# Expert rows fetched five units ahead into the row table's own tiles, half-block pairs ended one unit sooner, and the expert stage's pools laid out anew

## The chip, the cores and the metric

The kernel runs on one core of a Trainium2 chip. The time is the device time of one execution in microseconds. The kernel before was timed three times: 1548.76, 1552.86 and 1553.0 us, median 1552.86. The profile shown below comes from a further execution of 1552.57 us, with a span of 1550.8 us from its first to its last instruction; the profile's times count from the start of the span. TensorE is called PE, VectorE DVE, ScalarE ACT, GpSimd POOL and SyncE SP; SP issues most of the DMAs.

## The reference

The network has two layers on 2708 nodes with 256 features. Each layer is a graph attention, in layer 0 followed by causal self-attention, and then a mixture of eight experts in which every row goes to the two experts with the highest router probability. The expert part is what the change touches:

```python
h1 = jnp.einsum('nc,ehc->neh', flat, w1)
h3 = jnp.einsum('nc,ehc->neh', flat, w3)
h = jax.nn.silu(h1) * h3                       # hidden size 682
y = jnp.einsum('neh,ech->nec', h, w2)
out = jnp.einsum('ne,nec->nc', gates, y)       # gates: two non-zero per row, they sum to 1
x = x + out
```

Everything is computed in float32. The kernel computes only the two chosen experts of each row.

## The kernel before

**Order of the stages.** `network` calls `first` (graph attention, self-attention and routing of layer 0), `experts_blocks(0)`, `second` (graph attention and routing of layer 1) and `experts_blocks(1)`. In `first` and `second` the order of the instructions on each engine is written out by a planner (the class `Plan`, with lengths and ranks given for each step) and is kept as written. In `experts_blocks` the framework orders them: it goes through the program with estimated durations and, on each engine, takes the first instruction in program order whose needs it thinks are met. An engine, or a DMA queue, then works strictly in that order, and the order can differ from the program's by a whole expert.

**The table of rows.** `XR` holds 22 tiles of 128 rows. A row has 268 numbers: 256 features (`XB` is a view of these), the row's token number, eight gates and padding. While a layer is routed, each tile of `XR` is scattered to a table `xs` in DRAM (line 1808, by POOL, twice, once for each chosen expert). There every expert has its own region, with its rows packed in blocks of 128. When the last tile is scattered, `XR` has no more use until the next layer's routing, apart from the first few tiles: some blocks are worked on inside `first` and `second` while the routing still runs (`EARLY`: three blocks in layer 0, four in layer 1; `LATE`: two blocks of layer 0's last expert, worked on at the start of `second`). These early and late blocks are fetched into `XR[:, 0]` and the tiles after it, and run in `some_blocks` (lines 531 to 614).

**Units of an expert stage.** Each expert has five blocks (`NB`), which are worked on in units: a pair, a pair and a single block. Rows beyond five blocks are rare; they are cut in half blocks of 64 rows (`HALF_B`), and ten such half blocks of any experts (`MORE`) run as five half-block pairs, each one unit ahead of the pairs of experts 2 to 6. Which expert a half block belongs to is known only at run time: `table()` computes it on DVE, and SP reads it into registers for the fetch of its rows (line 2023) and for the load of its weights. In units, an expert in the middle of the stage is: half-block pair, pair, pair, single. Layer 0 has 14 pairs and 7 single blocks left for its stage, layer 1 has 15 and 6; the half-block pairs are 5 each.

**A unit, step by step.**

- `fetch` (lines 2023 and 2027): SP brings the unit's rows from `xs` to tiles `xt`, of which there are nine.
- `front` (lines 2041 to 2046): PE transposes the rows to PSUM, ACT copies them to `xTs`.
- `up` (lines 2061 to 2071): for six chunks of the hidden size, PE multiplies the transposed rows by w1 and w3 into a PSUM tile `pup` (five banks), ACT takes the silu of one half (`sl`), DVE multiplies it by the other into `hT`. Five chunks are 128 wide, the last has only 42 columns of each weight. There are three `hT` tiles.
- `down` (lines 2080 to 2086), one unit later: PE multiplies `hT` by w2 into a bank `y` (there are two), DVE multiplies by the gate into `ys`, and POOL adds the rows to the result in DRAM by an indirect accumulating DMA (`add_rows`, line 614). An add waits for the one before it.
- In a pair, the last chunks of the two blocks lie at partitions 0 to 63 and 64 to 127 of `hT`, and the last rows of w2 are loaded twice, so that the two last products each take 64 rows of PE (line 2083).
- A half-block pair does the same in `up_halves` (line 2099; rows 0 to 63 with one room's weights, 64 to 127 with another's), where a gate `gk` is computed with the product `gj` (line 2111) from the rows `xt` alone. Its hidden values come out untransposed (`hid`); `turn_halves` transposes them (line 2121) at the end of the next unit, and `down_halves` (line 2133) runs a unit after that and ends with two adds of 64 rows.

**Weights.** An expert's weights fill a room of 17 KB per partition. Three rooms rotate among the eight experts (two in `arena`, one called `room`), and two more (`more`) take the weights of a half-block pair. `load_expert` (lines 1983 to 1990) issues seven DMAs, three of 640 KB and four of 42 KB; the first use of a room also clears its padding on POOL (1975, 1976).

**Order of the work in the stage's loop.** For unit k the program emits: the load of an expert's room, the load of the two extra rooms (three units after a half-block pair began), the fetch of unit k + 2, the unit's own `up` or `up_halves`, the turn of an earlier half-block pair, the front of unit k + 2 and the down of unit k - 1.

**Where the tiles lie.** Pools of tiles stack in SBUF. After `arena` comes a place which the stages use in turn. In bytes per partition from there: in `first`, `X0` to 22.5 KB, the attention's pool to 78 KB, then a pool with the early blocks' `xTs` and `ys` to 95 KB; in `second`, `X1` to 22.5 KB, a pool `skeep` to 56 KB, and a pool `swork` with the blocks' `xTs`, `chunks` and `ys` to 95 KB. In `experts_blocks` the pool with `hT`, the three rooms and the small table tiles comes first, to 71.5 KB, and the pool with `xt`, `xTs`, `sl`, `ys` and `hid` follows to 101 KB. A tile may be written only when what lay in its place is no longer in use.

The two lines that say which rows a fetch takes and where it puts them are

```python
xt = sp.tile([P, ROW], F32, tag="xt", name="xt", bufs=9)
after_all(nc.sync.dma_start(out=xt, in_=xs[row:row + P, :]), xs)
```

where `after_all` makes the fetch wait for all scatters of the layer.

Of the kernel before, what the change touches and what calls it, by code (L numbers as in the profile page):

```python
# [24 lines left out]
NT = (N + P - 1) // P  # L25
# [5 lines left out]
NE = 8  # L31
HID = 682
NHC = (HID + P - 1) // P
HH = HID // 2
NF = HID // P
# [4 lines left out]
HALF_B = 64  # L40
MORE = 10
# [107 lines left out]
def adj_ffn_kernel(ctx, tc, x, adj, vecs, bias_rows, tab, w_gnn0, w_gnn1, wqkv, wo,  # L149
# [43 lines left out]
    make_identity(nc, ident)  # L193
    offdiag = const.tile([P, P], F32, name="offdiag")
# [1218 lines left out]
    def second(X, XB, xs0, x1, x2, sd, mb, xs, arena, load_weights):  # L1413
# [9 lines left out]
        with ExitStack() as s:  # L1423
# [8 lines left out]
            identb = keep.tile([P, P], BF16, name="identb")  # L1432
            nc.vector.tensor_copy(identb, ident)
# [537 lines left out]
    def load_expert(room, w1, w3, w2, e, used=False):  # L1971
        cut = NF * P
        a, b, c, d = weights_at(room)
        if not used:
            nc.gpsimd.memset(c, 0.0)
            nc.gpsimd.memset(d[:, NF, :], 0.0)
        if isinstance(e, int):
            w1v, w3v = (w[:, e, :].rearrange("(k p) h -> p k h", p=P) for w in (w1, w3))
            w2v = w2[e]
        else:  # L1980
            w1v, w3v = (w[:, bass.ds(e, 1), :].rearrange("(k p) o h -> p k (o h)", p=P) for w in (w1, w3))
            w2v = w2[bass.ds(e, 1)].rearrange("o h c -> (o h) c")
        nc.sync.dma_start(out=a, in_=w1v[:, :, :cut])
        nc.sync.dma_start(out=b, in_=w3v[:, :, :cut])
        nc.sync.dma_start(out=c[:, :, :REST], in_=w3v[:, :, cut:])
        nc.sync.dma_start(out=c[:, :, HIGH:], in_=w1v[:, :, cut:])
        nc.sync.dma_start(out=d[:, :NF, :], in_=w2v[:cut, :].rearrange("(k p) c -> p k c", p=P))

        for q in (0, HIGH):
            nc.sync.dma_start(out=d[q:q + REST, NF, :], in_=w2v[cut:, :])  # L1990

    def experts_blocks(layer, w1, w3, w2, xs, acc, arena):
# [8 lines left out]
        with ExitStack() as s:  # L2001
            keep = s.enter_context(tc.tile_pool(name=f"bkeep{layer}", bufs=1))
            hTs = [keep.tile([P, NHC, 2, P], F32, name=f"hT{i}") for i in range(3)]
            for hT in hTs:
                nc.gpsimd.memset(hT[:, NF, :, :], 0.0)
# [3 lines left out]
            with tc.tile_pool(name=f"slot{layer}", bufs=2) as sp, \  # L2009
                    tc.tile_pool(name=f"bpu{layer}", bufs=5, space=PSUM) as pu, \  # L2010
# [5 lines left out]
                def fetch(unit):  # L2016
                    xts = []
                    for e, j in unit:
                        xt = sp.tile([P, ROW], F32, tag="xt", name="xt", bufs=9)
# [30 lines left out]
                def up(k, w, xT, B):  # L2050

                    hT = hTs[k % len(hTs)]
                    for n in range(NHC):
                        pp = pu.tile([P, 2, 2, P], F32, tag="pp", name="pup")
# [12 lines left out]
                        else:  # L2067
                            nc.scalar.activation(sl[:REST, :B, :], pp[HIGH:HIGH + REST, 0, :B, :], AF.Silu)
                            for b in range(B):
                                q = HIGH * b  # L2070
                                nc.vector.tensor_tensor(hT[q:q + REST, n, b, :], sl[:REST, b, :],
                                                        pp[:REST, 0, b, :], ALU.mult)
                    return hT

                def down(e, w, hT, xts):

                    ys = [bank() for _ in xts]
                    for b, y in enumerate(ys):
                        for n in range(NF):
                            nc.tensor.matmul(y, hT[:, n, b, :], w[3][:, n, :], start=(n == 0), stop=False)  # L2080
                    for b, y in enumerate(ys):
                        part_ = slice(HIGH * b, HIGH * (b + 1)) if len(ys) > 1 else slice(0, P)
                        nc.tensor.matmul(y, hT[part_, NF, b, :], w[3][part_, NF, :], start=False, stop=True)  # L2083
# [106 lines left out]
                xt = [fetch(u) for u in units[:2]]  # L2190
                nxt = [front(x) for x in xt[:2]]
                asked, more_asked = 1, 0
                turns, downs = {}, {}
                for k, unit in enumerate(units):
                    e = unit[0][0]

                    if k == 0 or e is not None and e + 2 < NE and asked < e + 2 and units[k - 1][0][0] == e:
                        asked += 1
                        load_expert(rooms[asked % 3], w1, w3, w2, asked, asked > 2)
                    if k == 1:  # L2200
                        table()
                    if k == 2 or k > 2 and units[k - 3][0][0] is None and more_asked < MORE:
                        for room in more_rooms:
                            load_expert(room, w1, w3, w2, register(tab[0:1, 0, more_asked:more_asked + 1], NE - 1), more_asked > 1)
                            more_asked += 1
                    if k + 2 < len(units):
                        xt.append(fetch(units[k + 2]))
# [184 lines left out]
```

## Time and profile before

| What | Value |
|---|---|
| Time, median of three runs | 1552.86 us (1548.76 to 1553.0) |
| Time of the profiled execution | 1552.57 us |
| Its span, mean granted PE clock | 1550.8 us, 0.97 |
| Busy in the span: PE, DVE, ACT, POOL | 92%, 49%, 37%, 34% |
| First and last up product of layer 0's expert stage | 513.68 and 830.1 us |
| First and last up product of layer 1's expert stage | 1198.96 and 1522.7 us |
| DMA, mean over the span | 131 GB/s |

A page of the profile gives busy times and shares, the span in 40 slices of equal length (each digit is the busy share of a slice in tenths), the chain of work that ended last and the costliest groups of instructions. A line of the timeline has the start, the duration, the engine, the line of the kernel, the operation and the tiles written and read, and in brackets the time for which the engine had been idle and what ended it. A line of the waits has the instruction that waited, what it waited for, the total, the number of times and the longest. Where an instruction needed several things, the wait is put down to the one that came last.

### The profile page before, as it was taken

What the parts mean: (1) busy time and instruction counts of PE and PEld (TensorE: products, weight loads), DVE (VectorE), ACT (ScalarE), POOL (GpSimd) and SP (SyncE); (2) the same over time, 40 slices, a digit from 0 to 9 for tenths busy, and PEclk for the clock granted to TensorE, in tenths of its full rate; (3) what the DMA queues carried; (4) which work ended last, traced back from release to release, by engine and by line L of the source; (5) the groups of instructions that cost most, each with busy time, mean ns of one, the idle gap of its engine ahead of it and who ended that gap; (6) DMA issues with size and microseconds to landing.
All of it is one profiled execution on the core that took longest, in us unless ns stands there. A gap on an engine that the chain in (4) does not pass through costs nothing. (4 is left out here: it accounts for less than half of the span.)

```text
span 1550.8 us, 21255 instructions
## 1 busy us (share of the span) xinstructions
PE 1430.0 (92%) x7488; PEld 1025.5 (66%) x7488; DVE 760.8 (49%) x1670; ACT 566.8 (37%) x1134; POOL 530.9 (34%) x687
## 2 busy tenths in 40 slices
PE   6788898999999899989997899999997999999994
PEld 5533433433437687877786778888767877777883
DVE  5778999956684222221221564767654222122221
ACT  3577776764543122221221453443431212121210
POOL 5677679681063021212122210030444012211221
PEclk9999999999999899999999999999998999999998
DMA  7589667410013653565522751451413737454411
GB/s 262 191 280 303 224 222 230 163 60 8 7 58 92 191 149 104 143 179 168 135 30 43 170 113 34 99 125 48 151 58 99 227 98 205 138 161 121 111 25 19
DMA packets 200537, 203.40 MB, mean 131 GB/s; under 512 B 93752, under 2 KB 170536, under 8 KB 197712
## 3 DMA queue, kind: packets, MB, share of 16 engines
q1 hardware_dynamic: 175798, 172.51, 36.0%
q0 software_dynamic: 20352, 25.85, 9.4%
q10 hardware_dynamic: 4270, 3.58, 0.7%
q8 instruction: 61, 1.00, 0.3%
q14 instruction: 56, 0.46, 0.1%
HBM read 130.01 MB, written 56.37 MB: 120 GB/s over the span
## 5 line engine op out<-in xcount | busy, mean ns | idle before, releaser
L2061 PE MATMUL pup<-xTs,arena 128*128 128x256 f32 (+2 forms) x1320 | 257.9, 354 | 10.3 <-DVE hT L2066 9.6
L2061 PEld LDWEIGHTS pup<-xTs,arena 128*128 128x128 f32 (+1 forms) x1320 | 220.8, 191 | 43.5 <-DVE hT L2066 11.2
L1581 PE MATMUL po<-hb,PT 128*128 128x257 f32 (+2 forms) x968 | 226.0, 387 | 3.2 <-DVE PT L1574 3.2
L2065 ACT ACTIVATE sl<-pup 128x256 f32<-128x256 f32 (+1 forms) x210 | 73.2, 350 | 393.5 <-PE pup L2061 359.9
L1581 PEld LDWEIGHTS po<-hb,PT 128*128 128x128 f32 (+2 forms) x968 | 176.0, 188 | 42.1 <-issue 12.7
L2066 DVE TENSOR_TENSOR hT<-sl,pup 128x256 f32<-128x256 f32 (+1 forms) x210 | 77.6, 379 | 203.5 <-ACT sl L2065 197.3
L1103 ACT ACTIVATE e<-stt 128x1024 f32<-128x1024 f32 (+1 forms) x132 | 125.6, 986 | 94.8 <-PE stt L1097 65.6
L1142 DVE TENSOR_TENSOR es<-es,e 128x1024 f32<-128x1024 f32 x104 | 136.5, 1312 | 29.4 <-ACT e L1103 21.9
L614 POOL DMA_INDIRECT out<-ys,xt x41 | 63.0, 1536 | 252.1 <-DVE ys L2086 146.3
L614 POOL DMA_INDIRECT acc<-ys,xt x40 | 61.7, 1543 | 248.7 <-DVE ys L2086 149.3
L1097 PE MATMUL stt<-qT,kT 64*128 64x512 f32 (+1 forms) x528 | 132.8, 612 | 5.2 <-ACT e L1103 4.6
L1808 POOL DMA_INDIRECT xs<-XR,place x88 | 93.1, 1058 | 91.5 <-DVE mk L1568 39.2
L1123 PE MATMUL o<-e,V 128*64 128x512 f32 (+1 forms) x528 | 123.0, 589 | 0.0
L2080 PE MATMUL y<-arena,hT 128*128 128x256 f32 x510 | 115.2, 380 | 1.1 <-DVE ys L2086 1.1
L1559 ACT ACTIVATE E<-sb,dcol 128x768 f32<-128x768 f32 (+1 forms) x88 | 75.3, 860 | 110.9 <-DVE PT L1574 109.1
L2061 PE MATMUL pup<-xTs,room 128*128 128x256 f32 (+3 forms) x528 | 104.3, 354 | 5.5 <-DVE hT L2066 5.5
L2086 DVE TENSOR_SCALAR ys<-y,xt 128x256 f32<-128x256 f32 x71 | 31.7, 480 | 152.6 <-PE y L2083 152.5
L2080 PEld LDWEIGHTS y<-arena,hT 128*128 128x128 f32 x510 | 94.7, 190 | 13.7 <-DVE ys L2086 1.9
L2061 PEld LDWEIGHTS pup<-xTs,room 128*128 128x128 f32 (+1 forms) x528 | 87.3, 193 | 19.0 <-DVE hT L2066 6.3
L1097 PEld LDWEIGHTS stt<-qT,kT 64*128 64x128 f32 x528 | 44.5, 187 | 78.0 <-issue 63.4
L1123 PEld LDWEIGHTS o<-e,V 128*64 128x64 f32 x528 | 32.9, 137 | 70.1 <-issue 53.7
L971 DVE MAX8 tops<-arena 128x8 f32<-128x2708 f32 (+1 forms) x22 | 65.3, 2969 | 1.2 <-DMA arena<-in_adj 1.2
(322 smaller groups left out, 2088.7 us busy)
## 6 DMA issues: line engine op xcount, KB each, us to landing
more<-in_w SPq DMA_DIRECT2D x60, 640.0 KB
arena<-in_adj SPq DMA_DIRECT2D x21, 1354.0 KB
arena<-in_w SPq DMA_DIRECT2D x36, 640.0 KB
mb<-mb SPq DMA_DIRECT2D x44, 352.0 KB
xt<-xs SPq DMA_DIRECT2D x71, 134.0 KB
xs<-none SPq DMA_DIRECT2D x16, 536.0 KB
room<-in_w SPq DMA_DIRECT2D x12, 640.0 KB
more<-in_w SPq DMA_DIRECT2D x80, 42.0 KB
```

Source lines behind the costliest of these rows:

```text
L614: nc.gpsimd.indirect_dma_start(out=acc[:, :], out_offset=bass.IndirectOffsetOnAxis(ap=tokens.bitcast(I32), axis=0), in_=ys, in_offset=None ...
L1097: nc.tensor.matmul(st[:r, g, c0(sb):], kT[a:b, sb * P:sb * P + r], qT[a:b, t0 + (sb == t0 + 1):t0 + 2, :, :], start=True, stop=True)
L1103: nc.scalar.activation(e[:r, :, c0(sb):], v[sb, "st"][:r, :, c0(sb):], AF.Exp, scale=1.0 / HD ** 0.5)
L1123: nc.tensor.matmul(v["o"][g * HD:(g + 1) * HD, c:], V[:r, sb, g * HD:(g + 1) * HD], v[sb][:r, g, c:], start=(n + i == 0), stop=(n + i == t ...
L1142: nc.vector.tensor_tensor(es, es, v[sb][:r, :, c:], ALU.add)
L1559: nc.scalar.activation(e[:q, :n], sb[:q, i0:i1], AF.Exp, bias=dcol[:q, j:j + 1], scale=SLOPE - 1.0)
L1581: nc.tensor.matmul(v["po", i][:r, :F], v["PT", j][:q, a:a + r], hb[:q, j, :], start=(j == 0), stop=(j == NT - 1))
L1808: i = nc.gpsimd.indirect_dma_start(out=xs[:, :], out_offset=bass.IndirectOffsetOnAxis(ap=at, axis=0), in_=src, in_offset=None)
L2061: nc.tensor.matmul(pp[:to, i, :B, :], wn[:, c, :], xT[:, c, :B, :], start=(c == 0), stop=(c == KC - 1))
L2065: nc.scalar.activation(sl[:, :B, :], pp[:, 0, :B, :], AF.Silu)
L2066: nc.vector.tensor_tensor(hT[:, n, :B, :], sl[:, :B, :], pp[:, 1, :B, :], ALU.mult)
L2080: nc.tensor.matmul(y, hT[:, n, b, :], w[3][:, n, :], start=(n == 0), stop=False)
```

## The change

- `fetch` has no tiles of its own any more. It puts the rows into `XR[:, 5]` to `XR[:, 21]` in rotation, seventeen tiles.
- At the start three units are fetched, at unit 1 (after `table()`) units 3 to 5, and from then on unit k + 5 at unit k.
- The two extra rooms are loaded from unit 1 on, and again two units after a half-block pair began. These loads stand ahead of an expert's own load.
- A half-block pair is turned inside the next unit, between the third and the fourth chunk of its up products, and its `down_halves` runs at the end of that unit.
- In a pair the last chunk is no longer split: both blocks' last chunks lie at partitions 0 to 41, DVE multiplies them in one instruction, and each of the two last down products takes all 128 rows of PE, in a row with the other five. The second copy of w2's last rows is not loaded.
- The pool with `xTs`, `sl`, `ys` and `hid` is opened first and also holds the `hT` tiles; the pool with the rooms and the small tiles follows. The padding of `hT` is cleared on DVE, not on POOL.
- `identb`, used in `second`, is made once at the start and lies with the constants.

```diff
+    identb = const.tile([P, P], BF16, name="identb")
+    nc.vector.tensor_copy(identb, ident)
...
-            identb = keep.tile([P, P], BF16, name="identb")
-            nc.vector.tensor_copy(identb, ident)
...
-        for q in (0, HIGH):
-            nc.sync.dma_start(out=d[q:q + REST, NF, :], in_=w2v[cut:, :])
+        nc.sync.dma_start(out=d[:REST, NF, :], in_=w2v[cut:, :])
...
+            sp = s.enter_context(tc.tile_pool(name=f"slot{layer}", bufs=2))
+            hTs = [sp.tile([P, NHC, 2, P], F32, name=f"hT{i}", bufs=1) for i in range(3)]
+            for hT in hTs:
+                nc.vector.memset(hT[:, NF, :, :], 0.0)
             keep = s.enter_context(tc.tile_pool(name=f"bkeep{layer}", bufs=1))
-            hTs = [keep.tile([P, NHC, 2, P], F32, name=f"hT{i}") for i in range(3)]
-            for hT in hTs:
-                nc.gpsimd.memset(hT[:, NF, :, :], 0.0)
...
+            ring = [XR[:, t, :] for t in range(AHEAD, NT)]
...
-                        xt = sp.tile([P, ROW], F32, tag="xt", name="xt", bufs=9)
+                        xt = ring.pop(0)
+                        ring.append(xt)
...
-                def up(k, w, xT, B):
+                def up(k, w, xT, B, between):
 
                     hT = hTs[k % len(hTs)]
                     for n in range(NHC):
+                        if n == NHC // 2:
+                            between()
...
-                            for b in range(B):
-                                q = HIGH * b
-                                nc.vector.tensor_tensor(hT[q:q + REST, n, b, :], sl[:REST, b, :],
-                                                        pp[:REST, 0, b, :], ALU.mult)
+                            nc.vector.tensor_tensor(hT[:REST, n, :B, :], sl[:REST, :B, :], pp[:REST, 0, :B, :], ALU.mult)
...
                     for b, y in enumerate(ys):
-                        for n in range(NF):
-                            nc.tensor.matmul(y, hT[:, n, b, :], w[3][:, n, :], start=(n == 0), stop=False)
-                    for b, y in enumerate(ys):
-                        part_ = slice(HIGH * b, HIGH * (b + 1)) if len(ys) > 1 else slice(0, P)
-                        nc.tensor.matmul(y, hT[part_, NF, b, :], w[3][part_, NF, :], start=False, stop=True)
+                        for n in range(NHC):
+                            nc.tensor.matmul(y, hT[:, n, b, :], w[3][:, n, :], start=(n == 0), stop=(n == NHC - 1))
...
-                xt = [fetch(u) for u in units[:2]]
+                xt = [fetch(u) for u in units[:3]]
                 nxt = [front(x) for x in xt[:2]]
                 asked, more_asked = 1, 0
-                turns, downs = {}, {}
+                waiting, downs = [], {}
                 for k, unit in enumerate(units):
                     e = unit[0][0]
+                    if k == 1:
+                        table()
+                        xt += [fetch(u) for u in units[3:AHEAD + 1]]
+
+
+                    if more_asked < MORE and (k == 1 or k > 1 and units[k - 2][0][0] is None):
+                        for room in more_rooms:
+                            load_expert(room, w1, w3, w2, register(tab[0:1, 0, more_asked:more_asked + 1], NE - 1), more_asked > 1)
+                            more_asked += 1
                     if k == 0 or e is not None and e + 2 < NE and asked < e + 2 and units[k - 1][0][0] == e:
                         asked += 1
                         load_expert(rooms[asked % 3], w1, w3, w2, asked, asked > 2)
-                    if k == 1:
-                        table()
-                    if k == 2 or k > 2 and units[k - 3][0][0] is None and more_asked < MORE:
-                        for room in more_rooms:
-                            load_expert(room, w1, w3, w2, register(tab[0:1, 0, more_asked:more_asked + 1], NE - 1), more_asked > 1)
-                            more_asked += 1
-                    if k + 2 < len(units):
-                        xt.append(fetch(units[k + 2]))
+                    if k and k + AHEAD < len(units):
+                        xt.append(fetch(units[k + AHEAD]))
...
-                        turns[k + 1] = (k, hid, we, xt[k][0], gk)
+                        waiting.append((k, hid, we, xt[k][0], gk))
                     else:
+                        def between():
+                            while waiting:
+                                of, hid, wm, x, gk = waiting.pop()
+                                downs.setdefault(k, []).append((down_halves, wm, turn_halves(of, hid), x, gk))
+
                         we = weights_at(rooms[e % 3])
-                        hT = up(k, we, nxt[k], len(unit))
+                        hT = up(k, we, nxt[k], len(unit), between)
                         downs.setdefault(k + 1, []).append((down, e, we, hT, xt[k]))
-                    if k in turns:
-                        of, hid, we, x, gk = turns[k]
-                        downs.setdefault(k + 1, []).append((down_halves, we, turn_halves(of, hid), x, gk))
```

More of the change, by code (lines that the diff above doesn't have):

```diff
@@ L40 @@
 HALF_B = 64
+AHEAD = 5
 MORE = 10
@@ L1987, in load_expert @@
         nc.sync.dma_start(out=d[:, :NF, :], in_=w2v[:cut, :].rearrange("(k p) c -> p k c", p=P))
-        for q in (0, HIGH):
-            nc.sync.dma_start(out=d[q:q + REST, NF, :], in_=w2v[cut:, :])
+        nc.sync.dma_start(out=d[:REST, NF, :], in_=w2v[cut:, :])
     def experts_blocks(layer, w1, w3, w2, xs, acc, arena):
         with ExitStack() as s:
+            sp = s.enter_context(tc.tile_pool(name=f"slot{layer}", bufs=2))
+            hTs = [sp.tile([P, NHC, 2, P], F32, name=f"hT{i}", bufs=1) for i in range(3)]
+            for hT in hTs:
+                nc.vector.memset(hT[:, NF, :, :], 0.0)
             keep = s.enter_context(tc.tile_pool(name=f"bkeep{layer}", bufs=1))
-            hTs = [keep.tile([P, NHC, 2, P], F32, name=f"hT{i}") for i in range(3)]
-            for hT in hTs:
-                nc.gpsimd.memset(hT[:, NF, :, :], 0.0)
             rooms = [arena[:, :WE], arena[:, WE:], keep.tile([P, WE], F32, name="room")]
             more_rooms = [keep.tile([P, WE], F32, name=f"more{i}") for i in range(2)]
-            with tc.tile_pool(name=f"slot{layer}", bufs=2) as sp, \
-                    tc.tile_pool(name=f"bpu{layer}", bufs=5, space=PSUM) as pu, \
+            ring = [XR[:, t, :] for t in range(AHEAD, NT)]
+            with tc.tile_pool(name=f"bpu{layer}", bufs=5, space=PSUM) as pu, \
                     tc.tile_pool(name=f"bpt{layer}", bufs=1, space=PSUM) as pt_:
```

## The prediction

> **What bounds the kernel now.** I read the page first: TensorE is busy for 92% of the span and nothing else comes near, and its clock dips in only a few slices.
>
> ```profile
> span 1550.8 us, 21255 instructions
> PE 1430.0 (92%) x7488; PEld 1025.5 (66%) x7488; DVE 760.8 (49%) x1670; ACT 566.8 (37%) x1134; POOL 530.9 (34%) x687
> ...
> PE   6788898999999899989997899999997999999994
> ...
> PEclk9999999999999899999999999999998999999998
> ```
>
> So the time is PE's work, plus the holes in it. The two expert stages are 513.7 to 838.5 and 1198.96 to 1531.1. I took PE's waits there (500 to 860, then 1150 to 1551):
>
> ```profile
> PE pup L2061 <- DVE hT L2066: 7.5, 3, 3.9
> PE up L558 <- ACT xTs L543: 7.3, 1, 7.3
> PE pt L2041 <- DMA xt<-xs: 6.8, 1, 6.8
> ...
> PE pup L2061 <- DVE hT L2066: 7.6, 3, 3.1
> PE pt L2041 <- DMA xt<-xs: 6.4, 2, 6.2
> ```
>
> Three kinds of hole, the first two in both layers. I looked at each in the timeline.
>
> **Hole 1, the half-block gate.** One of the six, in the timeline of all engines (start, duration, and in brackets the idle time before and what ended it):
>
> ```profile
> 678.57 1.50 SPq L2023 DMA_DIRECT2D xt<-xs  x2
> ...
> 682.20 0.17 DVE L2111 SCALAR_TENSOR_TENSOR gj<-mown,xt 128x8 f32<-128x8 f32 x1 [11.13 <-DMA xt<-xs]
> ...
> 682.59 1.75 DVE L2066 TENSOR_TENSOR hT<-sl,pup 128x256 f32<-128x256 f32 x5
> ...
> 683.06 2.04 PE L2061 MATMUL pup<-xTs,arena 128*106 128x256 f32 x4 [3.88 <-DVE hT L2066]
> ```
>
> The product gj, which needs only a half block's rows, sits in DVE's order a whole expert before it is used, where its rows were supposed to have landed. They are fetched at 678.57, so DVE stands 11.13 us, five products hT pile up, the five banks of pup fill, and PE stops for 3.88 us. DVE waits of 8.48 us cost PE 1.24, so some 7.2 us of a DVE wait is free. SP's fetch is late because its tile (nine of them) is freed by an add to DRAM, and the adds are behind:
>
> ```profile
> 601.52 1.55 POOL L614 DMA_INDIRECT acc<-ys,xt  x1 [22.61 <-DVE ys L2086]
> 605.97 1.56 POOL L614 DMA_INDIRECT acc<-ys,xt  x1 [2.90 <-DVE hT L2066]
> 612.23 1.44 POOL L614 DMA_INDIRECT acc<-ys,xt  x1 [4.70 <-issue]
> 618.21 1.41 POOL L614 DMA_INDIRECT acc<-ys,upper  x1 [4.54 <-DMA acc<-ys,xt]
> 622.99 1.56 POOL L614 DMA_INDIRECT acc<-ys,xt  x1 [3.38 <-DVE ys L2086]
> ```
>
> Adds follow each other at 4.5 to 6 us. POOL idled 22.6 us, then got a pair's two adds and the half pair's two together, so the next pair's ys (ready at 614.4 to 615.3) was added only at 622.99. SP's own waits show L2027 139.5 us and L2023 23.0 us behind these adds in layer 0.
>
> **Holes 2 and 3, between stages.** The start of layer 1's stage, then the end of layer 0's:
>
> ```profile
> 1193.20 0.82 POOL L2005 MEMSET hT<- 128x256 f32 x3 [2.35 <-DMA out<-ys,XR]
> 1193.37 1.77 SPq L2027 DMA_DIRECT2D xt<-xs  x4
> 1195.74 0.66 PE L2041 MATMUL pt<-ident,xt 128*128 128x128 f32 x2 [6.23 <-DMA xt<-xs]
> ```
>
> ```profile
> 849.18 1.14 ACT L543 ACTIVATE xTs<-pt,vec 128x128 f32<-128x128 f32 x4 [18.73 <-POOL chunks L564]
> 849.60 10.44 PE L558 MATMUL up<-xTs,arena 128*128 128x128 f32 x76 [7.28 <-ACT xTs L543]
> ```
>
> The first fetch of a stage waits for the last early block's add, though it has no data from it. So does the memset of hT, which lies over X: a tile waits for all of an old pool that its own pool overlaps. At the end, xTs of the late blocks waits likewise for the stage's last add.
>
> **What the Trainium skill says.** "DMA: Bandwidth & Descriptors", section "Anatomy of one DMA — SWDGE (gpsimd) path": DMA engines don't wait on semaphores, the issuing sequencer does, so a fetch that waits holds all behind it on SP; and a DMA carries some 2.0 us of fixed time, mostly completion. The trace agrees: adds take 1.55 us of POOL and 2.9 until the next goes, a fetch 2.3 us (509.67 to 511.98). The same page, "Rules for kernel authors": accumulates to the same bytes must wait for one another; here that is the adds' spacing. "TensorE: Matmul & The Clock Gate", "HAM oscillation": long PE gaps bring a slow clock. Here four passes of the 106-wide chunk took 1.11 us after a gap of 1.24 and 2.04 after 2.39 to 3.88. Its Part 3, "The mechanism": matmuls in different row groups of the array overlap, which the change gives up; here the four 64-row passes of a pair take 0.63 us (600.02 to 600.65), four full ones 0.86 (2 x 0.43, from 574.20 to 574.63).
>
> **The change, part by part.**
>
> *Fetches in XR's tiles 5 to 21, three units at once and then five ahead; half pairs end within the next unit.* A fetch now waits for the add seventeen blocks back, not nine. And a half pair's adds come a unit (some 15 us) earlier, in POOL's empty 22.6 us, so the four adds no longer arrive together. Either alone should bring the 8.5 to 11 us DVE waits under the free 7.2. What they cost: the first pair of an expert takes 10.37 us undisturbed (574.63 to 585.00, before the next unit's first pass). With the stall, layer 0: 11.86, 15.90, 14.52, so 1.5 + 5.5 + 4.15 = 11.2. Layer 1: 12.73 less 0.3 for the flag's matmul, 14.88, 15.43, and 10.95 against 9.66 for the next unit on a slow clock: 2.1 + 4.5 + 5.1 + 1.3 = 13.0. Together 24.2; bounds 0 and 24.2 (a stall that grows is the slower rival below). I take 22. The half pair's turn moves to mid-unit: six transposes (0.82), as before; it takes two of five banks, of which about two are in use. down_halves now meets no down before it, so its wait of 0.15 for a y bank goes, ten times: -1.5.
>
> *Start of the stages.* The XR tiles belong to no new pool, so the fetch waits for the row scatters alone (landed by 504.7, where two fetches went out at once), not for 509.67. Layer 0: fetch 504.7, rows 507.2, transposes and xTs 1.7 (511.98 to 513.68), first up at about 509.1 instead of 513.68: -4.6. Layer 1: last scatter 1182.02, rows by 1187.5; PE's early block ends at 1188.5, its bank is read by 1189.0; from there 2.4 us of transposes and copies (3.2 before, 0.8 of it waiting for rows): 1191.4 instead of 1198.96, -7.6. With no gap the first unit runs at 9.66 instead of 10.85: -1.2. Sum -13.4; the bound the other way is 0, if xTs still waits. It should not: the new slot pool (hT 18.4 KB, xTs 6.1, sl 3.1, ys 4.1, hid 6.1) fills 38 KB from X's place, short of the work pool with ys. I take -13. The rooms and the table now lie over that pool, which adds waits in layer 0: room's memsets (POOL; next behind them an add at 542.7) and loads (SP; behind them the table's fetch and the extra rooms' loads) go from 488 to after 509.6, for a use at 574.6; the table's 3.6 us of DVE (505.70 to 509.33) start at 509.6, with the first hT behind it, within the free 7.2. Uncovered, each us late is one on PE. On SP up to fifteen fetches of some 0.44 us move ahead of the weights: 6.6 us, covered as below.
>
> *End of layer 0.* swork of the next stage overlaps the rooms, no longer ys: ACT goes at 842.4, not 849.18, so the late blocks' up starts 6.7 us earlier. They free X's fourth load (876.72) and the second half of the mask transposes (878.65 to 890.4), for which DVE waits until 893.38 and PE until 895.12. X's first loads don't move (848.9), nor does the first mask half, on SP until 863.1; so 0 to 8, I take -5.5.
>
> *Down.* A pair's last chunks are whole: 29 pairs (15 in layer 1, 14 in layer 0). Now 595.61 to 600.65, 5.04; two single blocks 2 x 2.60 (572.03 to 574.63): 5.20. +0.16 x 29 = +4.6, all on PE.
>
> *Nothing:* one load of 42 KB less in each of 36 (0.45 us of SP each); one product of 42x256 for two (0.57 on DVE, which waits for PE); identb to the constants (0.22); hT's memsets on DVE, not POOL: no such row, POOL 0.3 to 0.9, DVE's 128x256 at most 0.48, three in its idle time (at worst 1.4 a layer ahead of the routing; at best the same off nothing).
>
> Sum: -22 - 1.5 - 13 - 5.5 + 4.6 = -37.4. The profiled execution took 1552.57 (span 1550.8), 0.3 under the median of 1552.86: 1515.2.
>
> **Rivals.** *The stall stays (0.17).* gj is still put right behind the supposed landing of its fetch; further ahead, it only stalls somewhere else. For: fetches already ran as far ahead as the tiles let them. Against: the adds' queue empties. 1552.6 - (37.4 - 22) = 1537.
> *The starts stay (0.10).* xTs or its bank waits for the add after all, and the late blocks' gain is met by X's loads: 1552.6 - 22 - 1.5 + 4.6 = 1534.
> *Slower (0.08): the half blocks' weights come late.* Now the second room's load goes out at 608.2 to 613 for a use at 614.3, and in layer 1 a room, both extra rooms (2.1 MB each: three of 640 KB, four of 42) and seventeen tiles of rows (134 KB each), 8.5 MB, come in one burst at the start. Ten half units, each PE's loss: from 3.7 us each it eats the gain; 5 us give 1552.6 - 37.4 + 50 = 1565. Against: down_halves, which frees them, comes 15 us sooner, and DMA moved 288 GB/s in 1200 to 1220, so 8.5 MB in 30 us from 1193, before the first half unit at about 1232 (1239.92 less 7.6).
> *No change (0.03)* would need the first two rivals at once, 1552.6 - 1.5 + 4.6 = 1556, or near it.
>
> **The numbers.** Likeliest, 0.62: 1515; its own range 1507 (all 24.2, 15, 8) to 1527. With the two faster rivals the range is 1506 to 1540, leaving out some 0.15. A measurement here tells 0.3%, some 4.7 us: faster 0.89, same 0.03, slower 0.08.
>
> **What would show it.** gj's idle time behind DMA near 0 and no PE wait on hT; the waits of fetches on adds gone; first up of the stages 4 and 7 us after the early block's y; ACT L543 without its wait; the pair's down 5.2. Wrong if PE waits appear at the half units' first matmul (weights), or at hT in other places.

## The result and the profile after

The changed kernel took 1505.98 us (median of four runs, 1502.83 to 1507.84), the kernel before, beside it, 1552.93 (1548.76 to 1561.73). The ratio is 0.9688, with a 95% interval from 0.9644 to 0.9733. The forecast was 1515 with a range from 1506 to 1540, and the result lies just under its lower end: the direction and the likeliest case were right, the gain was larger than the sum said. Timed again later, beside a kernel before of 1556.28 us, the changed kernel took 1502.19. The profiled execution took 1506.29 us, with a span of 1504.5.

The head of the page after, with busy time and share of each engine, TensorE's busy slices and its clock:

```profile
span 1504.5 us, 21112 instructions
PE 1417.7 (94%) x7488; PEld 1030.2 (68%) x7488; DVE 762.5 (51%) x1647; ACT 567.4 (38%) x1134; POOL 529.9 (35%) x681
...
PE   5878989989999999999999989999999999999995
...
PEclk9999999999999999999999999999999999999998
```

PE has the same 7488 products. It is busy 12.3 us less (1430.0 before): 8.6 of this fall in the two expert stages, mostly passes on a slow clock, which are gone, and 3.1 before 502 us, where the change does nothing. The other 34 us of span are holes that were closed. The slices of the two expert stages are all nines now.

PE's waits in layer 0's stage and its end (500 to 860), then in layer 1's (1150 to 1505); the columns are the total, the number and the longest:

```profile
PE pt L2043 <- DMA XR<-xs: 1.9, 2, 1.6
...
PE pup L2065 <- ACT xTs L2048: 0.6, 1, 0.6
...
PE up L561 <- ACT xTs L546: 0.3, 1, 0.3
...
PE pt L2043 <- ACT xTs L2045: 0.8, 1, 0.8
```

Nothing waits for `hT` any more (7.5 and 7.6 us before). The late blocks' up products wait 0.3 us for `xTs` instead of 7.3, the first transposes 1.9 and 0 us for rows instead of 6.8 and 6.4.

The timeline of the changed kernel, all engines, at the places that the prediction showed: a half block's fetch and its gate `gj`, the end of layer 0, the start of layer 1's stage.

```profile
637.61 1.56 SPq L2025 DMA_DIRECT2D XR<-xs  x2
...
645.39 0.17 DVE L2108 SCALAR_TENSOR_TENSOR gj<-mown,XR 128x8 f32<-128x8 f32 x1 [3.55 <-DMA XR<-xs]
...
825.51 1.14 ACT L546 ACTIVATE xTs<-pt,vec 128x128 f32<-128x128 f32 x4 [11.13 <-PE pt L539]
...
1160.27 7.00 SPq L2029 DMA_DIRECT2D XR<-xs  x15
...
1166.31 0.64 PE L2043 MATMUL pt<-ident,XR 128*128 128x128 f32 x4
```

DVE still stands at `gj`, 3.55 us here, and PE doesn't notice. ACT copies the late blocks as soon as PE has transposed them. In layer 1 fifteen fetches go out before the last early block's down products (at 1162.67), and PE's transposes follow its last work without a wait for rows.

Where the 46.3 us of span went, each length taken between the same two instructions in both profiled executions (each at its start, unless its end is named):

| Stretch | Before | After | Difference |
|---|---|---|---|
| layer 0: last early down to the stage's first up product | 11.37 | 6.50 | -4.9 |
| layer 0's expert stage, to the first product after its last down | 325.5 | 313.6 | -11.9 |
| from there through `second` to the last early down of layer 1 | 346.5 | 340.15 | -6.4 |
| layer 1: last early down to the stage's first up product | 13.24 | 5.56 | -7.7 |
| layer 1's expert stage, to the end of its last down | 332.1 | 317.6 | -14.5 |
| from there to the end of the span | 19.7 | 18.6 | -1.1 |

Below, "cycle" is the time from one half-block pair's first product to the next one's. In an expert without a stall it was 46.68 us before (48.17 from 614.30 to 662.47, less a stall of 1.49); the stalled ones had 48.2 to 53.0. After, five of the eight are 46.72 or 46.73, and the other three hold the products that check the flags.

### The profile page after: what moved, and what is told of

Same layout as the page of the kernel before. It is cut to its first block, busy times and chain, and to the rows that moved or that the text cites. A ratio compares the mean times of both kernels' runs of the same rounds, so it can differ in the third digit from the quotient of the medians.

```text
span 1504.5 us, 21112 instructions
## 1 busy us (share of the span) xinstructions
PE 1417.7 (94%) x7488; PEld 1030.2 (68%) x7488; DVE 762.5 (51%) x1647; ACT 567.4 (38%) x1134; POOL 529.9 (35%) x681
## 3 DMA queue, kind: packets, MB, share of 16 engines
q1 hardware_dynamic: 173782, 170.96, 37.4%
## 5 line engine op out<-in xcount | busy, mean ns | idle before, releaser
L2065 PE MATMUL pup<-xTs,arena 128*128 128x256 f32 (+2 forms) x1320 | 252.8, 350 | 0.6 <-ACT xTs L2048 0.6
L1582 PEld LDWEIGHTS po<-hb,PT 128*128 128x128 f32 (+2 forms) x968 | 177.3, 189 | 44.0 <-issue 13.1
L617 POOL DMA_INDIRECT out<-ys,XR x45 | 69.4, 1542 | 246.7 <-DVE ys L2083 110.0
L617 POOL DMA_INDIRECT acc<-ys,XR x45 | 69.8, 1552 | 226.3 <-DVE ys L2083 94.5
L2080 PE MATMUL y<-arena,hT 128*128 128x256 f32 x612 | 136.7, 379 | 0.0
L1809 POOL DMA_INDIRECT xs<-XR,place x88 | 93.4, 1061 | 92.8 <-DVE mk L1569 41.3
L2080 PEld LDWEIGHTS y<-arena,hT 128*128 128x128 f32 x612 | 114.3, 190 | 14.5
L2083 DVE TENSOR_SCALAR ys<-y,XR 128x256 f32<-128x256 f32 x71 | 34.3, 484 | 141.2 <-PE y L2080 141.1
L2065 PE MATMUL pup<-xTs,room 128*128 128x256 f32 (+3 forms) x528 | 99.9, 346 | 0.0
```

The source lines that it names most:

```text
L617: nc.gpsimd.indirect_dma_start(out=acc[:, :], out_offset=bass.IndirectOffsetOnAxis(ap=tokens.bitcast(I32), axis=0), in_=ys, in_offset=None ...
L1582: nc.tensor.matmul(v["po", i][:r, :F], v["PT", j][:q, a:a + r], hb[:q, j, :], start=(j == 0), stop=(j == NT - 1))
L1809: i = nc.gpsimd.indirect_dma_start(out=xs[:, :], out_offset=bass.IndirectOffsetOnAxis(ap=at, axis=0), in_=src, in_offset=None)
L2065: nc.tensor.matmul(pp[:to, i, :B, :], wn[:, c, :], xT[:, c, :B, :], start=(c == 0), stop=(c == KC - 1))
```

## The experiments

**Only the half pairs' end moved.** The kernel before with the turn inside the next unit; nine row tiles, the fetch two units ahead, pools and split chunks as before.

```diff
-                        hT = up(k, we, nxt[k], len(unit))
+                        def between():
+                            while waiting:
+                                of, hid, wm, x, gk = waiting.pop()
+                                downs.setdefault(k, []).append((down_halves, wm, turn_halves(of, hid), x, gk))
+
+                        hT = up(k, we, nxt[k], len(unit), between)
...
-                    if k in turns:
-                        of, hid, we, x, gk = turns[k]
-                        downs.setdefault(k + 1, []).append((down_halves, we, turn_halves(of, hid), x, gk))
```

> The kernel before, with one part of the change: half-block pairs are turned and ended within the next unit. Nine row tiles, the fetch two units ahead, the pools and the split last chunk stay. Theory (either part alone cures the stall): the half pair's two adds no longer come together with a pair's two, fetches go out earlier, gj waits less than the 7 us that PE can bear: no wait of PE on hT, 24 us for the stall and some 3 us for down_halves between whole units, so 1552.9 - 27 = 1526 us. Rival (the distance of the fetch alone matters): PE still waits on hT for more than 10 us in all, 1540 to 1550 us.

Measured: 1525.78 us (1525.43 to 1529.57), ratio 0.9828 (0.9802 to 0.9854). No wait of PE on `hT` in either layer, and all cycles from the second half pair on are 46.46 or 46.47, but for the one with the flags' products in layer 1. `gj` still waits for its rows, 13.0 us in four waits in layer 0 and 14.9 in four in layer 1 (31.4 and 36.2 before). The longest, on DVE:

```profile
1238.39 0.17 DVE L2113 SCALAR_TENSOR_TENSOR gj<-mown,xt 128x8 f32<-128x8 f32 x1 [6.64 <-DMA xt<-xs]
```

A DVE wait of 6.64 us costs PE nothing, one of 8.48 cost 1.24 in the kernel before: the prediction's free 7.2 us lies between them. This one part does away with the whole stall. It also shows the stall's true size. Both stages together are 26.8 us shorter than before; half pairs without a stall account for ten times 0.21 (cycles of 47.58 and 50.14 became 47.36 and 49.92), so the stall, with the slow clock that it left behind, was 24.7. (In the kernel before 0.7 of it are two half pairs whose weights came late, of which more below.)

**Only the rows fetched further ahead.** The kernel before with `XR`'s tiles 5 to 21 and five units' lead; turns, pools and split chunks as before.

```diff
-                        xt = sp.tile([P, ROW], F32, tag="xt", name="xt", bufs=9)
+                        xt = ring.pop(0)
+                        ring.append(xt)
...
-                    if k + 2 < len(units):
-                        xt.append(fetch(units[k + 2]))
+                    if k and k + AHEAD < len(units):
+                        xt.append(fetch(units[k + AHEAD]))
```

> The kernel before, with one part of the change: rows fetched five units ahead into seventeen of XR's tiles. Half pairs end two units later as before, pools and split last chunk as before. Theory (either part alone cures the stall): the fetch of a half block stands behind an add seventeen blocks back, no wait of PE on hT: 24 us less; and at the starts of the stages the rows are there early, but xTs still lies over the early blocks' pool and waits for the last early add, so of the 13 us some 4 come: 1552.9 - 28 = 1525 us. Rival (only the adds' order matters): PE still waits on hT, 1540 to 1549 us. Rival on the starts (the fetch alone brings them all): 1552.9 - 37 = 1516 us.

Measured: 1529.23 us (1526.95 to 1530.59), ratio 0.9841 (0.9816 to 0.9866). Again no wait of PE on `hT`; `gj` waits 10.0 and 8.9 us in three waits each, at most 4.6. The starts are 9.7 and 10.0 us instead of 11.4 and 13.2: 4.9 us of the gain come from the fetch alone, and what stays is ACT's copy to `xTs`, which has then been idle for 10.7 and 9.9 us, until the early block's add has landed. The median is 4 us above the 1525 expected. In the trace 2.8 of it are seen: PE waits 2.0 us once for a flag (`bad`), and one cycle of layer 0 is 0.8 us longer than its neighbours. DVE's order shows what stands ahead of both:

```profile
673.97 0.15 DVE L2141 COPY upper<-XR 64x1 int32<-64x1 int32 x1 [8.93 <-DMA acc<-ys,upper]
674.67 4.55 PE L2064 MATMUL pup<-xTs,arena 128*128 128x256 f32 x20 [0.57 <-DVE hid L2110]
...
1285.75 0.15 DVE L2141 COPY upper<-XR 64x1 int32<-64x1 int32 x1 [6.30 <-DMA out<-ys,upper]
1287.43 0.57 PE L2335 MATMUL y<-bad,allones 128*128 128x176 f32 x2 [2.02 <-DVE bad L2329]
```

The copy `upper` of a half pair's row numbers is now placed too early in the same way as `gj`: it waits six times for an add of a half block (41.3 us in all), and two of these waits reach PE. (Two others, of 8.15 and 7.98 us, don't: how much of a DVE wait is free depends on where in the unit DVE stands.) So either part alone ends the waits on `hT`, but the early fetch alone moves a small part of the stall to another early instruction. With the turn moved as well, in the changed kernel, `upper` has no such wait.

**The stall by its cause alone.** The kernel before, with `gj` and the copy `upper` held back on DVE until the half pair is turned: they write a tile which DVE first fills from the turned `hT`. Nothing else moves; the rows are as late as before.

```diff
-                    return hid, gk
+                    return hid, pair
...
-                def down_halves(w, hT, xt, gk):
+                def down_halves(w, hT, xt, pair):
+                    small = sp.tile([P, NE + 2], F32, tag="gj", name="gj")
+                    nc.vector.tensor_copy(small, hT[:, 0, 0, :NE + 2])
+                    gj, gk, upper = small[:, :NE], small[:, NE:NE + 1], small[:, NE + 1:]
+                    nc.vector.scalar_tensor_tensor(gj, own[:, pair, :], 1.0, xt[:, C + 1:C + 1 + NE],
+                                                   ALU.mult, ALU.mult, accum_out=gk)
```

> The kernel before, its fetches, turns, pools and split chunks kept; only gj and the copy upper are held back on DVE until the half pair is turned (they write a tile into which DVE first copies ten columns of the turned hT: ten small copies more). Fetches stay as late as before. Theory (the stall is nothing but DVE's order: a product that needs late rows, placed a whole expert too early): no wait of PE on hT, the cycles of an expert 46.7 us, 24.7 us less: 1553 - 24.7 = 1528 us. Rival (the late rows are then missed somewhere else, at PE's transposes of the half block or in the adds): PE waits on rows, 1540 to 1550 us.

Measured: 1531.8 us (1527.65 to 1533.94), ratio 0.9842 (0.9812 to 0.9872). Its timeline at the half block whose fetch stopped PE for 3.88 us in the kernel before:

```profile
678.61 1.50 SPq L2023 DMA_DIRECT2D xt<-xs  x2
...
682.05 9.66 PE L2061 MATMUL pup<-xTs,arena 128*128 128x256 f32 x44
...
682.99 0.17 DVE L2129 SCALAR_TENSOR_TENSOR gj<-mown,xt 128x8 f32<-128x8 f32 x1
```

The fetch goes out at 678.61, in the kernel before at 678.57: as late as ever. PE runs through its 44 products in 9.66 us, and `gj` comes after the turn, with its rows long there. So the late rows by themselves stop PE nowhere in the stages. What cost was an instruction placed ahead of where it was needed, in an engine that works in order. But the two stages are only 21.0 us shorter than before, and the median is 3.8 above the 1528 expected. Six half pairs take 4.95 to 5.71 us instead of 4.89, 2.5 more in all, at a full granted clock (1.00), and both first units ran on a slower clock than before, 1.35 in all. In three of the six the trace names the half block's weights as the cause: PE waits for their DMA. In SP's queue these loads stand behind fetches that wait. One of the three, SP and the weight loads of PE:

```profile
637.27 17.31 SPq L2027 DMA_DIRECT2D xt<-xs  x3
...
660.17 3.04 SPq L1990 DMA_DIRECT2D more<-in_w  x2
...
663.78 0.25 PEld L2099 LDWEIGHTS pup<-more,xTs 128*64 128x64 f32 x4 [0.60 <-DMA more<-in_w]
```

The three fetches keep SP for 17 us, and the last loads of the second room go out at 660.17 for a half pair that begins at 662.98. How much of the 2.5 us is the fetches' doing was not tested; the half pair before, which holds the rooms until its down (649.98 to 652.79), may have a share. At most it is a tenth of what the order on DVE cost. Three quite different edits (order on DVE, order of the adds, distance of the fetch) each end PE's waits on `hT`.

**The pools in their old order.** The changed kernel, but with `hT`, rooms and table first and cleared on POOL.

```diff
-            sp = s.enter_context(tc.tile_pool(name=f"slot{layer}", bufs=2))
-            hTs = [sp.tile([P, NHC, 2, P], F32, name=f"hT{i}", bufs=1) for i in range(3)]
-            for hT in hTs:
-                nc.vector.memset(hT[:, NF, :, :], 0.0)
             keep = s.enter_context(tc.tile_pool(name=f"bkeep{layer}", bufs=1))
+            hTs = [keep.tile([P, NHC, 2, P], F32, name=f"hT{i}") for i in range(3)]
+            for hT in hTs:
+                nc.gpsimd.memset(hT[:, NF, :, :], 0.0)
```

> The changed kernel with the pools in their old order (hT, rooms and table first, the pool of xTs and ys after it), hT cleared on POOL; all else as changed. Theory (the layout brings the starts and the end of layer 0): xTs waits for the last early add again and the late blocks' xTs for the last add of layer 0: PE waits some 7 us at the first late up product; 1506 + 9 (what is left of 13 with early rows) + 6.4 = about 1521 us. Rival (the rows' own tiles bring the starts): only the end of layer 0 is lost, 1512 us.

Measured: 1519.29 us (1515.88 to 1522.33), ratio 0.9771 (0.9742 to 0.9801). From the first half pair on, the stages are the changed kernel's to 0.01 us in every cycle. The holes are back, at the starts of both stages and at the end of layer 0. The last two:

```profile
833.07 1.14 ACT L546 ACTIVATE xTs<-pt,vec 128x128 f32<-128x128 f32 x4 [16.66 <-POOL chunks L567]
...
1180.00 0.58 ACT L2045 COPY xTs<-pt 128x512 f32<-128x512 f32 x1 [9.97 <-DMA out<-ys,XR]
1180.64 0.71 PEld L2043 LDWEIGHTS pt<-ident,XR 128*128 128x128 f32 x4 [5.09 <-ACT xTs L2045]
```

The rows are there (PE transposed the first at 1175.14), but the copy out of PSUM waits for the early block's add. The start of layer 1's stage is 10.0 us here, 5.56 in the changed kernel and 13.2 in the one before: the rows' own tiles bring 3.2 of the 7.7, the layout 4.5. The 76 late up products take 11.59 us after their wait of 5.82, against 8.78 in the changed kernel: on a slow clock behind the wait.

**The split last chunk restored.** The changed kernel with the last chunks of a pair at partitions 0 and 64 again, and w2's last rows loaded twice.

```diff
-                        for n in range(NHC):
-                            nc.tensor.matmul(y, hT[:, n, b, :], w[3][:, n, :], start=(n == 0), stop=(n == NHC - 1))
+                        for n in range(NF):
+                            nc.tensor.matmul(y, hT[:, n, b, :], w[3][:, n, :], start=(n == 0), stop=False)
+                    for b, y in enumerate(ys):
+                        part_ = slice(HIGH * b, HIGH * (b + 1)) if len(ys) > 1 else slice(0, P)
+                        nc.tensor.matmul(y, hT[part_, NF, b, :], w[3][part_, NF, :], start=False, stop=True)
```

> The changed kernel with the split last chunk of a pair restored (42 rows at partitions 0 and 64, two products on DVE, w2's last rows loaded twice); all else as changed. By the prediction's term (0.16 us for each of 29 pairs, nothing else): 1506 - 4.6 = 1501.4 us. By what the trace after shows (0.13 to 0.24 for each pair, 4.9 in all, but the two ys of a pair come 2.6 us apart, which saves two bank waits of 0.65 and 1.1 us in the last adds): 1506 - 2.5 = 1503.5 us. Rival (two adds at once bring the stall back): PE waits on hT, over 1510 us.

Measured: 1502.79 us (1500.25 to 1504.55), ratio 0.9668 (0.9642 to 0.9693). No wait of PE on `hT`, so the rival is out; the time can't tell the other two figures apart, and the traces have to. PE's timeline around two pairs, first of this kernel, then of the changed one:

```profile
640.68 4.48 PE L2084 MATMUL y<-arena,hT 128*128 128x256 f32 x20
645.10 0.70 PE L2087 MATMUL y<-arena,hT 64*128 64x256 f32 x4
645.73 5.17 PE L2066 MATMUL pup<-xTs,arena 128*128 128x128 f32 x44
650.73 0.60 PE L2044 MATMUL pt<-ident,XR 128*128 128x128 f32 x4
```

```profile
641.03 5.35 PE L2080 MATMUL y<-arena,hT 128*128 128x256 f32 x24
646.21 5.06 PE L2065 MATMUL pup<-xTs,arena 128*128 128x128 f32 x44
651.11 0.60 PE L2043 MATMUL pt<-ident,XR 128*128 128x128 f32 x4
```

Split, the down takes 5.05 us from start to start and the up after it 5.00; whole, 5.18 and 4.90. So 0.10 of the 0.13 that the split saves is lost in the next products, where PE goes back from 64 rows to 128. The net price of a whole chunk is 0.03 us. Only ahead of a half pair, whose products use 64 of PE's columns, is it more: the half pair starts 5.05 us after a split down and 5.28 after a whole one, and is no faster for it. A cycle, with one pair of each sort, is 46.47 split and 46.73 whole, so 0.23 to 0.24 there. For 19 and 10 pairs that makes 3.0 us. Against it stand, in the same traces, the end of each stage (72.77 us split from the last half pair on, 72.23 whole, though its three pairs cost 0.09 more: 0.63 for the bank wait, twice) and the last adds: 19.9 us from the last down to the end of the span instead of 18.6. By the traces whole chunks cost some 0.4 us in all, or 0.6 with the 1.1 us by which the last stretch differs from that of the kernel before. This last part is uncertain: over all runs the stretch took 18.6 to 20.4 us where the last pair was whole, 19.7 to 20.6 where it was split. Layer 1's stage, without it, is 317.65 us whole (317.64 when repeated) and 316.80 split: 0.85 for 15 pairs, where 0.16 each would make 2.4.

**Once more, and two attempts on what is left.** The changed kernel again, word for word, on one chip with two more: the split in all pairs but the last of each stage (there the second block's last chunk runs on 64 rows, but right behind its other five), and the same with the last pair's down in the middle of the last single block's up.

```diff
+                        whole = k >= len(units) - 2
...
+                        if not split:
+                            part_ = slice(0, HIGH) if b else slice(0, P)
+                            nc.tensor.matmul(y, hT[part_, NF, b, :], w[3][part_, NF, :], start=False, stop=True)
...
+                            if k == len(units) - 1:
+                                for f, *args in downs.pop(k, ()):
+                                    f(*args)
```

> The changed kernel once more, word for word, as the base for the next two on the same chip: 1506 us, within 3.

> The changed kernel with the split last chunk restored in all pairs but the last one of each stage, whose ys come apart as in the changed kernel. Theory (a whole chunk costs 0.13 us for a pair and gives back 0.95 us of bank waits at each stage's end and 1.3 us in the last adds): 27 x 0.13 = 3.5 us faster than the changed kernel, 1502.5 us, and some 2 to 3 us faster than the fully split one. Rival (the price of the whole chunk is the 4.6 us of the prediction, and nothing comes back): no faster than the fully split kernel.

> As the kernel with the split in all pairs but the last, and the last pair's down products stand in the middle of the last single block's up products, 2.5 us sooner. Theory (the last adds, 4.5 to 5.4 us apart, are in a row at the end of each stage): the last pair's adds go 2 us sooner, of which the tail of layer 1 gets 1.5 to 2 and the start of the next layer's loads as much: 3 us less, 1499.5 us. Rival (the adds are spaced by their own length and the single block's add is last anyway): no difference, 1502.5 us.

Measured: the changed kernel 1502.19 us (1499.82 to 1505.29), ratio 0.9659 (0.9635 to 0.9683); split but for the last pair 1500.13 (1497.23 to 1500.85), 0.9643 (0.9622 to 0.9665); last pair early 1500.87 (1499.88 to 1505.39), 0.9656 (0.9632 to 0.9680). The same kernel differs by 3.8 us between its two medians, so the 3.2 us between it and the split one of before are nothing, and no interval here is apart from another. From the traces: the cycles show 0.26 to 0.30 us each for the split, but each stage's stretch from the last half pair on is 0.3 longer, not shorter; the two stages together are 2.1 us shorter, apart from a slow clock in layer 0's first unit, where 3.5 was expected. The early last pair brings nothing, as its rival said: in both variants the last three adds follow two others without a pause, the first of the five issued 12.46 us ahead of the last down's end, and they come 4.4 to 5.6 us apart. The pair's results were early, but the adds ahead of them were not through. None of the variants is shown to beat the changed kernel.

## Why the mechanisms held, and where the sizes were off

The mechanisms stood, the sizes did not; the sum of the prediction was -37.4, the spans differ by 46.3. (Its own lower end of 1507 is 1.5 below what its terms give, 1552.6 - 24.2 - 1.5 - 15 - 8 + 4.6 = 1508.5.) Term by term:

| Term of the sum | Predicted | Measured | From |
|---|---|---|---|
| stall at `gj`, late half-block weights in it | -22 | -24.7 | the kernel with the turn alone, less half pairs |
| half pairs' down | -1.5 | -2.1 | ten cycles, 0.21 each |
| starts of the stages, with the clock behind | -13 | -13.6 | -4.9, -7.7, first units +0.2 and -1.2 |
| end of layer 0 | -5.5 | -6.4 | the table of stretches |
| whole last chunks | +4.6 | +0.6 | 19 x 0.03 + 10 x 0.24 - 2 x 0.63 - 1.1, the last uncertain |
| sum | -37.4 | -46.2 | |

**The step that failed** is the paragraph "Down". Its 0.16 for each of 29 pairs is 4.0 of the 8.8 us by which the sum was short. It timed the pair's down from its start to the start of the next products, and took its cost from two single blocks. But the cost of going to 64 rows and back lies in part behind that stretch: the next 44 passes take 9.76 or 5.17 us after a split pair, 9.66 or 5.06 to 5.07 after a whole one. Both could be read in the trace of before, here the up of a single block after a split pair and after a single block:

```profile
556.23 5.17 PE L2061 MATMUL pup<-xTs,arena 128*128 128x128 f32 x44
...
825.08 5.07 PE L2061 MATMUL pup<-xTs,arena 128*128 128x128 f32 x44
```

What a whole chunk cost in the runs is 0.03 us, or 0.24 ahead of a half pair, 3.0 in all, and at least 1.3 of that comes back at the ends of the stages. And the split finishes both `y` of a pair together. The kernel before shows what hangs on that: PE waits 0.57 us for a `y` bank at the end of either stage, and three adds stand in a row at the very end. I priced the edit by PE's passes alone, and gave no lower bound for what it would free. The prediction cited the Trainium skill, "TensorE: Matmul & The Clock Gate", Part 3, for matmuls that overlap in different row groups, "which the change gives up"; the overlap is seen here (four passes in 0.63 us), but in pairs with another pair or a single block behind them most of what it gave (0.10 of 0.13) was lost in the products that follow.

**The stall's discount** is 2.7 of it. The bound of 24.2 had been worked out, and 22 taken without a reason from the profile. All of it came, and 0.5 more. Most likely this is what the sum left out: the half pairs at 714.69 and 765.77 took 5.14 and 5.32 us instead of 4.89, 0.7 more. The granted clock was 1.00 in both; their weight loads waited for the extra rooms' DMAs, and the longest of these waits was:

```profile
766.21 0.19 PEld L2099 LDWEIGHTS pup<-more,xTs 128*64 128x64 f32 x3 [0.24 <-DMA more<-in_w]
```

In the kernel with the turn alone, and in the changed one, all ten take 4.89.

**The end of layer 0** was right in its chain: ACT goes at once, PE's late products start 7.0 us earlier after their transposes, X's fourth load 8.75 earlier (28.8 us after the product that follows the stage's last down, 37.5 before). It left out the clock: the late products take 8.78 us instead of 10.44. So 8.7 were gained there, of which this execution gave 2.3 back further on: PE still waits for the mask (3.95 us, 2.72 before) and its 14 products behind that took 5.94 us instead of 3.30. In the second execution of the same kernel the stretch is 337.2 us, not 340.15.

**The starts** came as worked out: first up products at 508.94 (about 509.1 predicted, with 0.1 us between the two executions), 7.7 us less in layer 1 (7.6), 9.66 us for the first unit there. That both parts are needed was not said: the rows' tiles without the layout bring 4.9 us of 12.6.

**What should be seen.** Right: no wait of PE on `hT`, ACT's wait gone, the pair's down at 5.18. The first up products come 3.7 and 2.8 us after the early block's last product (8.6 and 10.5 before), where the list said 4 and 7; the sum had it right. Wrong in two points, without a cost: `gj` still waits for its rows (6.4 and 7.0 us in all, at most 3.6), and SP's fetches still wait 100.4 and 99.1 us for adds. The queue is now so far ahead that PE doesn't feel these waits. The rivals: in the changed kernel the stall went nowhere else, the starts moved, and the half blocks' weights never kept PE waiting. The first and the last of them were not idle fears, though: with the fetch alone part of the stall went to `upper`, and with `gj` alone held back the weights came late.

## What to carry to other kernels

An instruction that a framework places by an estimate, in an engine that works in order, makes every late input a stall for all that stands behind it; look for what the waiting instruction is wanted for, and when, before making the input earlier. Price an edit on the tensor engine from one start to the next but one, with the operations that follow, and ask what is freed or bunched by its results; a saving of 0.13 us in the stretch itself was 0.03 over two. And a discount on a bound that was worked out from a trace needs a reason from the trace.

## What the runs showed of the hardware

- Going back from passes on 64 rows to passes on 128 cost PE about 0.10 us in the products behind: 44 passes of a single block took 5.17 us after a split pair and 5.06 after a whole one, of a pair 9.76 and 9.66. The same 9.76 stands behind a half pair's down, which uses 64 columns (in the changed kernel at 631.21). The loss is of the size of what 64-row passes save in a pair (0.13).
- TensorE's clock fell after idle times of less than 2 us each. At the start of layer 0's stage PE idles in two or three pieces. With 1.61, 0.33 and 0.56 us, and with 1.70, 0.44 and 0.56, the next two passes took 1.22 us and the 42 after the second transposes 10.98 and 9.81; with 1.61, 0.19 and 0.56, with 1.67 and 0.56, and with 1.66 and 0.56 they took 0.70 and 9.23. It isn't the sum of all pieces that counts: the granted clock goes from 1.00 to 0.50 at 507.5 in the first of these executions and at 508.2 in the second, before the last piece, with PE idle for 1.75 and 2.34 us of the 3.4 us ahead of it. What divides the five executions was not tested. The Trainium skill, "TensorE: Matmul & The Clock Gate", section "HAM oscillation", speaks of gaps above some 3.4 us; here the measurement decides.
- Accumulating adds to DRAM, one after the other, were issued 4.4 to 5.6 us apart at the end of all these kernels, and the span ended 13.1 to 13.2 us after the last one in the two main profiles.
